# 5120 small memsets on an idle GpSimd, beside a kernel that stores 520 MB

## The chip, the cores and the metric

One core of a Trainium2 chip (trn2) runs the kernel. The metric is device time in microseconds (us), and the figure quoted for a kernel is the median.

## The reference

For each of 4096 rows and each pair i < j of 32 fields of 64 numbers, field i is multiplied by the 64x64 matrix of that pair and then, number by number, by field j.

```python
vi = inputs[:, i_idx, :]            # 496 pairs i < j
vj = inputs[:, j_idx, :]
vdotw = jnp.einsum('bpd,pde->bpe', vi, W)
inter = vdotw * vj
return inter.reshape(B, -1)         # 4096 x 31744, float32: 520 MB
```

## The kernel before

All matrices stay in SBUF. For each of 32 tiles of 128 rows, x is loaded and transposed (ScalarE evicts the transposes), TensorE multiplies into PSUM, VectorE multiplies the PSUM result by x into a ring in SBUF, and SyncE issues four stores from the ring. GpSimd does nothing after the start.

```python
for t in range(NT):
    xt = xbuf[t % 2]
    if t + 1 < NT:
        load_x(t + 1)                     # one DMA on ScalarE's queue
    for s, group in enumerate(STORES):    # four stores a tile
        osb = ring[:, at : at + store_w[s]]
        ...
        for p in group:
            ...                           # transposes of the next x
            for c1 in range(first, width[2 * p] + 1, BANK):
                ...                       # 40 turns in a tile
                pm = take_banks(2)
                for h in range(1 + bool(odd)):
                    nc.tensor.matmul(pm[...], xT[...], w_sb[...], start=True, stop=True)
                nc.vector.tensor_tensor(osb..., pm..., xj, ALU.mult)
        nc.sync.dma_start(out=out[ts(t, P), o0 : o0 + store_w[s]], in_=osb)
```

Of the kernel before, what the change touches and what calls it, by code (L numbers as in the profile page):

```python
# [1 line left out]

# [6 lines left out]

F32 = mybir.dt.float32  # L10
ALU = mybir.AluOpType

P = 128
BANK = 512
BANKS = 8

STORES = [[0, 1], [2, 3], [4, 5, 6], [7, 8, 9, 10, 11, 12, 13, 14, 15]]

LOADS = [[0], [1], [2, 3], [4, 5, 6], [7, 8, 9, 10, 11, 12, 13, 14, 15]]


FIRST_HALF_AT, SECOND_HALF_AT = 9, 3
RING = 28160


@with_exitstack
def pair_bilinear_kernel(
    ctx: ExitStack,
    tc: tile.TileContext,
    x: bass.AP,  # L30
    w: bass.AP,
    out: bass.AP,
    F: int,
    D: int,
):























    nc = tc.nc
    NT = x.shape[0] // P  # L60
    NPR = F // 2

    width = [(F - 1 - i) * D for i in range(F)]
    off = [sum(width[:i]) for i in range(F)]


    woff = [i % 2 * D + sum(width[i % 2 : i : 2]) for i in range(F)]
    store_w = [sum(width[2 * p] + width[2 * p + 1] for p in g) for g in STORES]

    const = ctx.enter_context(tc.tile_pool(name="const", bufs=1))  # L70
    psum = ctx.enter_context(tc.tile_pool(name="ps", bufs=1, space=bass.MemoryType.PSUM))

    ident = const.tile([P, P], F32, tag="ident", name="ident")
    make_identity(nc, ident)

    def runs(tl, a, b, n):

        ap = tl[:, a : a + n]
        return bass.AP(ap.tensor, ap.offset, [list(ap.ap[0]), [b - a, 2], list(ap.ap[1])])

    xbuf = [const.tile([P, F * D], F32, tag=f"x{b}", name=f"x{b}") for b in range(2)]

    def load_x(t):
        nc.scalar.dma_start(out=xbuf[t % 2], in_=x[ts(t, P), :])

    pring = psum.tile([P, BANKS * BANK], F32, tag="pring", name="pring")
    bank = 0

    def take_banks(n):

        nonlocal bank
        if bank + n > BANKS:
            bank = 0
        got = pring[:, bank * BANK : (bank + n) * BANK]
        bank = (bank + n) % BANKS
        return got

    xT = const.tile([P, NPR * P], F32, tag="xT", name="xT")

    def transpose_x(xt, g):  # L100

        n = 2 * BANK // P
        pt = take_banks(2)
        for c in range(n):
            nc.tensor.transpose(pt[:, ts(c, P)], xt[:, ts(n * g + c, P)], ident)  # L105
        nc.scalar.copy(xT[:, ts(g, 2 * BANK)], pt)  # L106

    ring = const.tile([P, RING], F32, tag="ring", name="ring")
    at = 0

    load_x(0)
    w_sb = const.tile([P, sum(width[0::2])], F32, tag="w", name="w")
    done = 0
    for g in LOADS:

        upto = woff[2 * g[-1]] + width[2 * g[-1]]
        nc.sync.dma_start(out=w_sb[:, done:upto], in_=w[:, done:upto])
        done = upto

    transpose_x(xbuf[0], 0)  # L120
# [3 lines that stand above are left out]
            load_x(t + 1)  # L124
        for s, group in enumerate(STORES):
            if at + store_w[s] > RING:
                at = 0
            osb = ring[:, at : at + store_w[s]]
            at += store_w[s]
            o0 = off[2 * group[0]]  # L130
            for p in group:
                if p == SECOND_HALF_AT:
                    transpose_x(xt, 1)
                if p == FIRST_HALF_AT and t + 1 < NT:
                    transpose_x(xbuf[(t + 1) % 2], 0)
                first = (width[2 * p] - 1) % BANK + 1
                for c1 in range(first, width[2 * p] + 1, BANK):
                    n = first if c1 == first else BANK
                    c0 = c1 - n
                    odd = width[2 * p + 1] and c1 > D  # L140
                    pm = take_banks(2)
                    for h in range(1 + bool(odd)):
                        a = woff[2 * p + h] + c0 - h * D
                        nc.tensor.matmul(  # L144
                            pm[:, h * BANK : h * BANK + n],
                            xT[h * D : (h + 1) * D, ts(p, P)],
                            w_sb[h * D : (h + 1) * D, a : a + n],
                            start=True,
                            stop=True,
                        )  # L150
                    xj = xt[:, (2 * p + 1) * D + c0 : (2 * p + 1) * D + c1]
                    o = [off[2 * p + h] - o0 + c0 - h * D for h in range(2)]
                    if odd and (c0 or c1 < width[2 * p]):
                        nc.vector.tensor_tensor(  # L154
                            runs(osb, o[0], o[1], n),
                            runs(pm, 0, BANK, n),
                            bass.AP(xj.tensor, xj.offset, [xj.ap[0], [0, 2], xj.ap[1]]),
                            ALU.mult,
                        )
                    else:  # L160
                        for h in range(1 + bool(odd)):
                            nc.vector.tensor_tensor(  # L162
                                osb[:, o[h] + h * D : o[h] + n],
                                pm[:, h * (BANK + D) : h * BANK + n],
                                xj[:, h * D :],
                                ALU.mult,
                            )
            nc.sync.dma_start(out=out[ts(t, P), o0 : o0 + store_w[s]], in_=osb)


# [26 lines left out]
```

## Time and profile before

| | before |
|---|---|
| time | 1338.01 us (1337.81 to 1338.14) |
| VectorE busy | 1183.0 us, 89% |
| TensorE busy | 1164.7 us, 87% |
| GpSimd busy | 0.7 us |
| DMA engines | over 90% in 39 of 40 slices, 421 GB/s |
| VectorE waits for stores | 101.6 us |

A busy share near 90% on two engines is no bound while both wait. The row to look for is the one without gaps, and that is the transfers. The prediction below shows these lines. One view that it doesn't show is used later, the same kernel in three stretches of 408 us (columns: stretch, length, busy time and count of PE, PEld, DVE, ACT and POOL, then granted clock, DMA share, GB/s):

```profile
100.00:508.00 408.00, 360.62 (x1674) 172.59 (x1676) 367.39 (x429) 20.24 (x20) 0.00 (x0) 0.95 0.99 424
508.00:916.00 408.00, 363.75 (x1674) 175.35 (x1676) 367.64 (x428) 20.24 (x20) 0.00 (x0) 0.95 0.99 424
916.00:1324.00 408.00, 355.62 (x1644) 165.96 (x1640) 365.37 (x426) 19.23 (x19) 0.00 (x0) 0.97 0.99 423
```

### The profile page before, as it was taken

The numbers are of one execution on the slowest core, as the hardware profiler recorded it, in microseconds if no ns is written. First come the engines' busy times: TensorE is split into PE (matmuls) and PEld (weight loads), VectorE is DVE, ScalarE is ACT, GpSimd is POOL, SyncE is SP. The second block draws the span as 40 slices with busy tenths as digits, with TensorE's granted clock in tenths as the row PEclk, the third lists the DMA queues.
The fourth block names the chain that finished last, engine by engine and source line by source line (L and its number), as shares of the span: only waits on it lengthen the run. The fifth ranks groups of instructions, "written<-read, shape, count | busy, mean of one in ns | idle before, by whom it ended". The sixth has DMA issues, their size and how long they took to land.

```text
span 1336.3 us, 13134 instructions
## 1 busy us (share of the span) xinstructions
PE 1164.7 (87%) x5376; PEld 552.9 (41%) x5376; DVE 1183.0 (89%) x1376; ACT 66.1 (5%) x65; POOL 0.7 (0%) x6
## 2 busy tenths in 40 slices
PE   6988888988889888898888898888988888898893
PEld 3444344443444444344434444444444444443341
DVE  5999888989889988999988899888998888998894
ACT  0000000000000000000000000000000000000000
POOL 0000000000000000000000000000000000000000
PEclk9999999999999988998998999889988989999997
DMA  9999999999999999999999999999999999999998
GB/s 395 431 428 436 429 425 427 425 425 425 426 421 401 425 431 415 427 421 425 429 428 419 417 416 435 421 415 425 422 422 426 423 424 412 431 412 439 417 424 353
DMA packets 23820, 562.88 MB, mean 421 GB/s; under 512 B 2640, under 2 KB 2640, under 8 KB 2896
## 3 DMA queue, kind: packets, MB, share of 16 engines
q1 hardware_dynamic: 19152, 528.49, 92.6%
q10 hardware_dynamic: 4608, 33.56, 6.0%
q8 instruction: 42, 0.69, 0.2%
q14 instruction: 18, 0.15, 0.0%
HBM read 41.94 MB, written 520.09 MB: 421 GB/s over the span
## 4 chain that ended last, share of the span: by engine, by line
DMA 45%; DVE 36%; PE 9%; issue 8%; DVEq 0%; ACT 0%
DMA out_dram<-ring 45%; DVE ring L154 30%; PE pring L144 9%; DVE ring L162 5%; DMA x<-in_x_dram 1%; DVEq L154 0%; PE pring L105 0%; ACT xT L106 0%; DVEq L193 0%
## 5 line engine op out<-in xcount | busy, mean ns | idle before, releaser
L144 PE MATMUL pring<-w,xT 64*128 64x512 f32 (+4 forms) x4864 | 1102.6, 568 | 143.3 <-DVE ring L154 131.8
L154 DVE TENSOR_TENSOR ring<-pring,x 128x1024 f32<-128x1024 f32 (+3 forms) x1056 | 1104.6, 1107 | 135.3 <-DMA out_dram<-ring 101.6
L144 PEld LDWEIGHTS pring<-w,xT 64*128 64x128 f32 x4864 | 497.3, 194 | 706.5 <-DVE ring L154 508.4
L106 ACT COPY xT<-pring 128x1024 f32<-128x1024 f32 x64 | 64.8, 1012 | 1225.5 <-PE pring L105 1183.7
L162 DVE TENSOR_TENSOR ring<-pring,x 128x64 f32<-128x64 f32 (+3 forms) x320 | 97.6, 355 | 0.3
L105 PEld LDWEIGHTS pring<-ident,x 128*128 128x128 f32 x512 | 55.6, 142 | 57.1 <-DVE ring L154 48.5
L105 PE MATMUL pring<-ident,x 128*128 128x128 f32 x512 | 70.9, 282 | 8.7 <-DMA x<-in_x_dram 8.7
L106 ACT ACT_TABLE_LOAD x1 | 1.3, 1283 | 1.6 <-PEq L189 1.6
masks.py:199 POOL TENSOR_SCALAR_AFFINE_SELECT ident<-ident 128x128 f32<-128x128 f32 x1 | 0.3, 292 | 0.1
masks.py:197 POOL MEMSET ident<- 128x128 f32 x1 | 0.2, 204 | 0.3 <-POOLq L189 0.3
L189 POOL MEMSET const-bfloat16-1.0<- 128x1 bf16 x1 | 0.1, 101 | 0.0
L189 POOL MEMSET const-uint8-127<- 128x1 uint8 x1 | 0.1, 101 | 0.0
L189 POOL MEMSET const-float32-0.0<- 128x1 f32 x1 | 0.1, 98 | 0.2 <-issue 0.2
L189 POOL MEMSET const-float32-1.0<- 128x1 f32 x1 | 0.1, 98 | 0.0
## 6 DMA issues: line engine op xcount, KB each, us to landing
out_dram<-ring SPq DMA_DIRECT2D x32, 4896.0 KB, 19.5
out_dram<-ring SPq DMA_DIRECT2D x32, 3936.0 KB, 17.7
out_dram<-ring SPq DMA_DIRECT2D x32, 3776.0 KB, 19.6
out_dram<-ring SPq DMA_DIRECT2D x32, 3264.0 KB, 20.1
x<-in_x_dram ACTq DMA_DIRECT2D x32, 1024.0 KB, 18.1
w<-in_w_dram SPq DMA_DIRECT2D x1, 2592.0 KB, 26.1
w<-in_w_dram SPq DMA_DIRECT2D x1, 2016.0 KB, 19.8
w<-in_w_dram SPq DMA_DIRECT2D x1, 1664.0 KB, 15.5
```

The lines of the kernel that those rows point to most:

```text
L105: nc.tensor.transpose(pt[:, ts(c, P)], xt[:, ts(n * g + c, P)], ident)
L106: nc.scalar.copy(xT[:, ts(g, 2 * BANK)], pt)
L144: nc.tensor.matmul(pm[:, h * BANK : h * BANK + n], xT[h * D : (h + 1) * D, ts(p, P)], w_sb[h * D : (h + 1) * D, a : a + n], start=True, st ...
L154: nc.vector.tensor_tensor(runs(osb, o[0], o[1], n), runs(pm, 0, BANK, n), bass.AP(xj.tensor, xj.offset, [xj.ap[0], [0, 2], xj.ap[1]]), ALU ...
L162: nc.vector.tensor_tensor(osb[:, o[h] + h * D : o[h] + n], pm[:, h * (BANK + D) : h * BANK + n], xj[:, h * D :], ALU.mult,)
L189: nc = bacc.Bacc("TRN2", target_bir_lowering=False, num_devices=1)
```

## The change

Its intent is to give the idle engine work that no other engine depends on: four memsets of one spare column in each of the 1280 turns of the inner loop.

```diff
     ring = const.tile([P, RING], F32, tag="ring", name="ring")
+    spare = const.tile([P, 1], F32, tag="spare", name="spare")
...
                     pm = take_banks(2)
+                    for _ in range(4):
+                        nc.gpsimd.memset(spare, 0.0)
```

## The prediction

> **What bounds the kernel now.** I read the page from the top: busy shares, the slices, the chain that ended last, then the waits, and last a table of the four tiles around the middle.

> ```profile
> span 1336.3 us, 13134 instructions
> PE 1164.7 (87%) x5376; PEld 552.9 (41%) x5376; DVE 1183.0 (89%) x1376; ACT 66.1 (5%) x65; POOL 0.7 (0%) x6
> DMA  9999999999999999999999999999999999999998
> ...
> HBM read 41.94 MB, written 520.09 MB: 421 GB/s over the span
> DMA out_dram<-ring 45%; DVE ring L154 30%; PE pring L144 9%; DVE ring L162 5%; DMA x<-in_x_dram 1%; DVEq L154 0%; PE pring L105 0%; ACT xT L106 0%; DVEq L193 0%
> ```

> The DMA row is full in 39 of 40 slices, and no engine is. The chain that ended last spends 45% of the span in the stores of the ring and most of the rest in VectorE's products (L154 and L162): a product may overwrite a piece of the ring only when the store of that piece has landed. Who waits for whom, in the listing of waits:

> ```profile
> DVE ring L154 <- DMA out_dram<-ring: 101.6, 40, 4.1
> DVE ring L154 <- PE pring L144: 22.8, 16, 13.6
> ```

> VectorE waits 101.6 us in all for stores, in 40 waits of at most 4.1 us, and only 22.8 us for TensorE, of which 13.6 are the start. So the stores set the pace and VectorE is close behind. The stretches of 41 us, nearly one tile of 128 rows each, say it by tile (columns: stretch, length, busy time and count for PE, PEld, DVE, ACT and POOL, then clock, DMA share, GB/s):

> ```profile
> 641.00:682.00 41.00, 35.82 (x170) 15.95 (x168) 36.99 (x43) 2.02 (x2) 0.00 (x0) 1.00 1.01 430
> 723.00:764.00 41.00, 36.19 (x166) 18.42 (x166) 36.97 (x43) 2.02 (x2) 0.00 (x0) 0.92 0.99 422
> ```

> VectorE works 36.97 us of a tile's 41 and TensorE about 36. Each has 4 to 5 us of air in a tile, the transfers have none, GpSimd has all of it. The clock granted to TensorE moves between 0.92 and 1.00 without moving the tile. Only three things could therefore cost time: something that takes VectorE more than its air, something that slows the transfers, or GpSimd ending last.

> **What the change really issues.** In the built program, the streams of TensorE, VectorE, ScalarE and SyncE are instruction for instruction what they were, waits included. GpSimd gets 5120 memsets of 128x1 float32. "Without waiting" isn't what was built: 5119 of them wait for GpSimd's own semaphore to reach the count that the memset before them sets, because all write the same column. They wait for no other engine, and nobody waits for them but the barrier at the end. So they form one serial chain that starts at once and runs at its own pace, and the pace decides if it ends before the rest.

> **The pace of the chain.** GpSimd's timeline at the start has both cases:

> ```profile
> 0.24 0.10 POOL L189 MEMSET const-float32-0.0<- 128x1 f32 x1 [0.24 <-issue]
> 0.27 0.10 POOL L189 MEMSET const-float32-1.0<- 128x1 f32 x1
> 0.31 0.10 POOL L189 MEMSET const-bfloat16-1.0<- 128x1 bf16 x1
> 0.34 0.10 POOL L189 MEMSET const-uint8-127<- 128x1 uint8 x1
> 0.73 0.20 POOL masks.py:197 MEMSET ident<- 128x128 f32 x1 [0.29 <-POOLq L189]
> 1.01 0.29 POOL masks.py:199 TENSOR_SCALAR_AFFINE_SELECT ident<-ident 128x128 f32<-128x128 f32 x1
> ```

> Memsets without a wait start 0.03 us apart though each shows 0.10: they overlap, and 5120 of them would be gone in 5120 x 0.033 = 0.17 ms. The select in the last line waits for the memset above it, as each new memset waits for its predecessor: start to start 0.28 us for a memset of 0.20. A one-column memset is 0.10 shorter (0.10 against 0.20), so a step of the new chain should be 0.28 - 0.10 = 0.18 us. 5119 x 0.18 = 921 us, and with 1 us of start GpSimd is done at about 922 us, 414 us before the end. It would end last only with a step over 1335 / 5119 = 0.261 us. This estimate rests on one pair of instructions, the second of another kind and with a register move between; I give a step over 0.26 us some 4%.

> [...]

> [...]

> [...] 10752 instructions (5376 matmuls and 5376 weight loads) x 64 B = 688,128 B, which is the 0.69 MB in 42 packets of the first queue below.

> ```profile
> q8 instruction: 42, 0.69, 0.2%
> q14 instruction: 18, 0.15, 0.0%
> ```

> **The change part by part.** Removed: nothing. Moved: the resident weights by 32 bytes in SBUF, to make room for the column. They are loaded once[...]; 0 us.

> Added, busy time: 5120 x 0.10 = 512 us of GpSimd shown busy (38%), beside everything; 0 us on the path. With start and end of a memset overlapping nothing in the chain, that is what the page should count.

> Added, VectorE: 0 ns for each memset[...]. The air allows some: 101.6 us / 5120 = 19.8 ns for each memset before VectorE takes over as the bound.

> Added, transfers: 5120 x 64 B = 327,680 B of instructions, 0.06% of the 562.88 MB moved. At 421 GB/s this is 0.8 us if it spreads over the 16 DMA engines, and this is time on the path, since the transfers are the bound.

> Sum: 1337.94 + 0.8 = 1338.7 us, rounded to 1339.

> **The rivals.** First, the lock: each memset might hold VectorE off for its 0.10 us. Then VectorE gains 512 us, less the 102 it waits for stores: 410 us more, about 1748. [...] A partial form, say 30 ns each, makes 154 us, less 102: some 52 us, 1390. I give these 1.5% together.

> Second, GpSimd as the bound: a step of 0.30 us makes 5119 x 0.30 = 1536 us, and the kernel some 1540. [...]

> Third, one DMA engine rather than sixteen. The trace has the 16 landing marks of each transfer, one from each DMA engine: the last comes a median of 2.1 us after the fifteenth, while most of the others lie within 0.2 us. So one engine is behind, and a store has landed only when it has. In the trace before, an instruction packet of 8 KiB took 0.309 us in most cases; the new fetches are 40 of them, 12.4 us of one engine's time if they all use the same one. If that is another than the late engine, the time stays where it is; if it is the late one, it is +12 us at worst, 1350, still inside 2%. I take one chance in eight.

> Fourth, the clock: more engines at work could lower TensorE's granted clock. But TensorE at 36 of 41 us has room for over 10%, and the tiles above take the same 41 us at 0.92 and 1.00. 0 us.

> **Range and chances.** The unchanged core of the argument gives 1338 to 1340. Executions of the kernel before scatter by only 0.3 us[...]: low end 1336. The high end, 1346, takes in part of the third rival. Slower by over 2% (above 1364.7) needs the lock or a step over 0.26 us: 1.5 + 4, about 5%. Faster has no mechanism at all: 1%. Within 2%: 94%.

> **What would show it.** Right: POOL with 5126 instructions and near 512 us busy, its digits ending about slice 28 of 40 (922 / 33.4 us each); the product of 1024 columns still at 1217 ns; the waits of VectorE for stores still near 100 us; the instruction queue up by 0.33 MB. Wrong: POOL digits up to the last slice and a chain led by POOL (the step is too short here); L154 above 1217 ns with fewer waits for stores (the lock); 8 to 12 us more with L154 unchanged and more waiting for stores (the late DMA engine).

The 0 ns for VectorE stands as my guess, not shown before the result; the trace before couldn't test it, as GpSimd is idle there while VectorE works. "The lock" is my name for the rival that a memset holds VectorE off. The low end of 1336 is an allowance of mine. The 64 B of an instruction are the trace's: 0.69 MB for 10752 instructions. That a landing mark comes from one DMA engine is my reading: the trace before has 165 transfers and 2640 marks, 16 each.

## The result and the profile after

The changed kernel takes 1354.38 us (1354.19 to 1354.46), 16.4 us more than the 1338.01 of before. The ratio is 1.0122, with a 95% interval of 1.0105 to 1.014. The time lies within 2%, but outside the range of 1336 to 1346 that I had given.

The page of the changed kernel, the lines that answer to those shown of before:

```profile
span 1352.6 us, 18254 instructions
PE 1161.6 (86%) x5376; PEld 553.5 (41%) x5376; DVE 1182.5 (87%) x1376; ACT 66.1 (5%) x65; POOL 503.6 (37%) x5126
POOL 6666666666666666666666640000000000000000
q14 instruction: 58, 0.48, 0.1%
DMA out_dram<-ring 51%; DVE ring L159 29%; DVE ring L167 5%; PE pring L149 5%; POOL spare L146 0%; DVEq L159 0%; PE pring L107 0%; ACT xT L108 0%; DVEq L198 0%; POOL ident masks.py:199 0%; DVEq L167 0%; POOL ident masks.py:197 0%; POOLq L194 0%
```

GpSimd ends in slice 24 of 40, so it doesn't end last, and it is on 0% of the chain. The stores' share of the chain rose from 45% to 51%. L154 of before is L159 here. Its widest form, from the groups with shapes kept apart (row: busy us, mean ns, idle before), and the wait for stores, from the listing of waits (us in total, times, longest):

```profile
L159 DVE TENSOR_TENSOR ring<-pring,x 128x1024 f32<-128x1024 f32 x768 | 901.8, 1214 | 17.3 <-PE pring L149 4.2 <-DMA out_dram<-ring 2.1
DVE ring L159 <- DMA out_dram<-ring: 122.0, 45, 5.0
```

A product takes 1214 ns against 1217 before: VectorE isn't slowed. It waits 122.0 us for stores against 101.6, which is 20.4 us more; this is where the time shows up. The same three stretches as before:

```profile
100.00:508.00 408.00, 351.85 (x1634) 167.82 (x1634) 358.54 (x416) 20.24 (x20) 256.89 (x2615) 0.95 0.98 417
508.00:916.00 408.00, 355.32 (x1638) 171.21 (x1638) 361.41 (x423) 19.23 (x19) 183.82 (x1871) 0.95 0.98 415
916.00:1324.00 408.00, 361.86 (x1682) 171.91 (x1680) 369.43 (x432) 20.24 (x20) 0.00 (x0) 0.96 0.99 422
```

Look at the last column beside the POOL column. While the memsets run, the transfers move 415 to 417 GB/s instead of 424, and when they have ended, 422. The loss is 1.9% of some 800 us, 15 us. So while the memsets run it is the transfers that lose time, and not an engine's work. The granted clock is unchanged (0.954 over the run against 0.956).

GpSimd's timeline at the start gives the pace of the chain:

```profile
0.72 0.20 POOL masks.py:197 MEMSET ident<- 128x128 f32 x1 [0.29 <-POOLq L194]
0.87 0.10 POOL L146 MEMSET spare<- 128x1 f32 x1
1.00 0.29 POOL masks.py:199 TENSOR_SCALAR_AFFINE_SELECT ident<-ident 128x128 f32<-128x128 f32 x1
1.23 4.78 POOL L146 MEMSET spare<- 128x1 f32 x31
```

31 memsets take 4.78 us, 0.154 us each; over all of them the start-to-start spacing is 0.156 us, and the last starts at 799.8 us.

### The profile page after: what moved, and what is told of

Same layout as the page of the kernel before. It is cut to its first block, busy times and chain, and to the rows that moved or that the text cites. A ratio compares the mean times of both kernels' runs of the same rounds, so it can differ in the third digit from the quotient of the medians.

```text
span 1352.6 us, 18254 instructions
## 1 busy us (share of the span) xinstructions
PE 1161.6 (86%) x5376; PEld 553.5 (41%) x5376; DVE 1182.5 (87%) x1376; ACT 66.1 (5%) x65; POOL 503.6 (37%) x5126
## 2 busy tenths in 40 slices
DMA  9999999999999999999999999999999999999998
DMA packets 23860, 563.21 MB, mean 416 GB/s; under 512 B 2640, under 2 KB 2640, under 8 KB 2896
## 3 DMA queue, kind: packets, MB, share of 16 engines
q10 hardware_dynamic: 4608, 33.56, 5.9%
HBM read 41.94 MB, written 520.09 MB: 416 GB/s over the span
## 4 chain that ended last, share of the span: by engine, by line
DMA 51%; DVE 34%; issue 9%; PE 5%; POOL 0%; DVEq 0%; ACT 0%; POOLq 0%
DMA out_dram<-ring 51%; DVE ring L159 29%; DVE ring L167 5%; PE pring L149 5%; POOL spare L146 0%; DVEq L159 0%; PE pring L107 0%; ACT xT L108 0%; DVEq L198 0%; POOL ident masks.py:199 0%; DVEq L167 0%; POOL ident masks.py:197 0%; POOLq L194 0%
## 5 line engine op out<-in xcount | busy, mean ns | idle before, releaser
L159 DVE TENSOR_TENSOR ring<-pring,x 128x1024 f32<-128x1024 f32 (+3 forms) x1056 | 1103.5, 1105 | 150.9 <-DMA out_dram<-ring 122.0
L146 POOL MEMSET spare<- 128x1 f32 x5120 | 503.0, 98 | 295.8
```

Of the source, the lines that this page charges most:

```text
L146: nc.gpsimd.memset(spare, 0.0)
L159: nc.vector.tensor_tensor(runs(osb, o[0], o[1], n), runs(pm, 0, BANK, n), bass.AP(xj.tensor, xj.offset, [xj.ap[0], [0, 2], xj.ap[1]]), ALU ...
```

## The experiments

**The theories.** A: the 327,680 B of GpSimd instructions are fetched by the one DMA engine that is behind the others, and every store waits for it. B: GpSimd's writes to SBUF, or its being busy, disturb VectorE or the transfers. After the first four runs theory A became A2: each instruction that is executed, whatever it does, loads that one DMA engine. All runs gave correct results. Differences are against the median of the kernel before in the same group of runs: 1338.07, 1338.18, 1338.14 and 1338.17 us. Instructions that do nothing were to stand in for the memsets, but plain no-ops were gone from the built program; drains stay (run 13 has 18254 instructions, 5120 more than the 13134 of before), so drains were used.

**1. Instructions that write nothing (e1_pool_drain).**

```diff
-                        nc.gpsimd.memset(spare, 0.0)
+                        nc.gpsimd.drain()
```

> 5120 drains on GpSimd in place of the memsets: as many instructions to fetch, but nothing is written to SBUF and no semaphore is counted up. Theory A (the 327,680 B of GpSimd instructions are fetched by the DMA engine that is late anyway, and every store waits for it): about 1354 us, the same 16 us more (1350 to 1358), with the second instruction queue near 0.48 MB. Theory B (the writes to SBUF or the semaphore updates disturb VectorE or the transfers): 1338 to 1340 us.

Measured: 1350.50 us (1350.09 to 1350.78), 12.4 us more, ratio 1.0092. So most of the loss, 12.4 of 16.4 us, needs no write, no time that the page counts as busy on GpSimd (0.7 us, as before) and no semaphore: 2.43 ns for each drain. Theory B in its pure form falls.

**2. The same writes from a loop (e2_pool_loop).** Four columns, so that a turn needs no waits inside it, and one drain a turn to keep the turns apart. A copy from the identity matrix only sets the order at the start.

```diff
-                    for _ in range(4):
-                        nc.gpsimd.memset(spare, 0.0)
...
     transpose_x(xbuf[0], 0)
+    with tc.tile_critical():
+        with nc.gpsimd.Fori(0, 1280) as _i:
+            for c in range(4):
+                nc.gpsimd.memset(spare[:, c : c + 1], 0.0)
+            nc.gpsimd.drain()
```

> 5120 memsets of one column each, but in a loop of 1280 times four on GpSimd, so the instructions are fetched once. Theory A: 1338 to 1340 us, the second instruction queue back near 0.15 MB. Theory B: 1350 to 1358 us, since as much is written. If a loop turn fetches its instructions anew, the queue shows it and the run says nothing.

Measured: 1357.61 us (1357.51 to 1357.79), 19.5 us more, ratio 1.0147. From its page:

```profile
span 1355.6 us, 22106 instructions
q14 instruction: 18, 0.15, 0.0%
```

The instruction queue is back at 0.15 MB, so nothing was fetched anew, and still this is the dearest of the variants on GpSimd. Theory A falls: it isn't the fetched bytes. But the first line has 22106 instructions, 8972 more than before. A turn of the loop executes seven: four memsets, the drain, an addition and a branch, and 1280 x 7 = 8960. 19.5 us over 8972 is 2.18 ns, close to the 2.43 ns of a drain in the run above. That points to the number of executed instructions, and this became theory A2. The run doesn't separate the kinds: 5120 memsets at the 3.20 ns of the change and 1280 drains at 2.43 make 19.5 us as well, with nothing for the additions and branches. Against that reading, these memsets post no semaphore updates (the kept trace has 5945 in all, against 11059 in the changed kernel), and run 13 suggests that the update is a part of the 3.20.

**3. The same number on another engine (e3_sp_drain).**

```diff
-                        nc.gpsimd.memset(spare, 0.0)
+                        nc.sync.drain()
```

> 5120 drains on SyncE, 160 in each tile between the stores that it issues; GpSimd idle. Theory A in its wide form (all engines' instructions but TensorE's come over the same late DMA engine): about 1354 us. Theory A in its narrow form (each sequencer fetches over a DMA engine of its own, and GpSimd's is the late one): 1338 to 1342 us. Theory B: 1338 to 1342 us too.

Measured: 1373.09 us (1372.86 to 1373.30), 35.0 us more, ratio 1.0261, beyond either theory. This run isn't clean: with the drains in SyncE's stream, the scheduler put TensorE's instructions in another order. From the waits of this run:

```profile
DVE ring L159 <- PE pring L149: 48.6, 46, 13.6
```

VectorE waits 48.6 us for TensorE, against 22.8 before. How the 35 us divide between the drains and the new order stays open.

**4. Half the dose (e4_half).** `range(4)` becomes `range(2)`: 2560 memsets.

> 2560 memsets instead of 5120. Theory A and theory B both say half of the 16.4 us: 1346 us (1344 to 1348). If the loss does not scale (a shift in the phase of stores and products, or the place of the weights in SBUF), it is nearer to 1338 or to 1354.

Measured: 1345.92 us (1345.81 to 1346.14), 7.9 us more, ratio 1.0059. It scales: 3.07 ns for each memset here, 16.37 / 5120 = 3.20 ns in the full change. From a shift of phase or of addresses I would not expect a half.

**5. Few wide memsets (e5_wide).**

```diff
-    spare = const.tile([P, 1], F32, tag="spare", name="spare")
+    spare = const.tile([P, 2048], F32, tag="spare", name="spare")
...
         xt = xbuf[t % 2]
+        for _ in range(13):
+            nc.gpsimd.memset(spare, 0.0)
...
-                    for _ in range(4):
-                        nc.gpsimd.memset(spare, 0.0)
```

> 416 memsets of 2048 columns in place of 5120 of one: GpSimd is busy about as long (416 x 1.8 us = 0.75 ms) and writes 166 times as much into SBUF, with a twelfth of the instructions. Theory A2 (each instruction that is executed costs the transfers about 2.3 ns, by what it sends over the late DMA engine's path, whatever it does): 416 x 3.2 ns = 1.3 us, 1339 to 1341 us. Theory B (GpSimd's writes or its being busy disturb): at least 1350 us.

Measured: 1339.46 us (1339.38 to 1339.55), 1.3 us more, ratio 1.0010. The group of these memsets on the page:

```profile
L127 POOL MEMSET spare<- 128x2048 f32 x416 | 751.2, 1806 | 23.8
```

GpSimd is busy for 751.2 us, longer than in the change itself, and writes 166 times as much, and it costs 1.3 us: 3.08 ns for each of the 416, though the interval of the ratio, 0.9995 to 1.0025, takes in no change at all. This is the cleanest of the runs against theory B.

**6 and 7. Splitting the load of x (e6_x120, e7_x126).** The aim was to take load off some DMA engines. What the traces show of how a transfer is shared out: each of the 165 transfers of the kernel before leaves 16 packets of 4 bytes and 16 landing marks, 2640 of each. The extra loads of runs 9, 14 and 11 below, of 68, 85 and 34 rows, leave 4, 5 and 2 more small packets each: the page's packets under 512 B rise from 2640 to 2764, 2795 and 2702, which is by 31 x 4, 31 x 5 and 31 x 2. I read each of these packets as one DMA engine taking part. Which engines these are, no record names, and for runs 6, 7 and 10 no count is shown here. So the engine numbers in the expectations are labels of mine: 0 to k-1 are the k engines of one extra load, 15 or 14 and 15 those that the split was meant to relieve, 0 to 7 those meant to get a row more. That a smaller set is part of a larger one, and that the split relieves any engine, I assumed; it was not shown.

```diff
-        nc.scalar.dma_start(out=xbuf[t % 2], in_=x[ts(t, P), :])
+        for lo, hi in ((0, P),) if t < 2 else ((0, 120), (120, P)):
+            nc.scalar.dma_start(out=xbuf[t % 2][lo:hi, :], in_=x[t * P + lo : t * P + hi, :])
```

> The kernel before without memsets, but from the third tile on x is loaded as 120 rows and 8 rows. [...] Theory A2 with engine 15 as the late one: faster, 1310 to 1330 us. With one of 8 to 14 as the late one: 1338 us. With one of 0 to 7: 30 x 0.3 = 9 us more, 1347 us. If no engine is late by load: 1338 to 1347 us.

> As the run with 120 rows, with 126 rows[...] Late engine 14 or 15: faster, 1310 to 1330 us. Late engine another: 1345 to 1357 us.

The edit of the second run is the same, with 126 for 120. Measured: 1349.23 us (1349.05 to 1349.77) with 120 rows, 11.1 us more, ratio 1.0083; 1347.53 us (1347.29 to 1347.84) with 126, 9.4 us more, ratio 1.0070. Neither run is faster, so if the split relieved an engine, nothing was gained by it. As an estimate, a packet of 8 KB, one row of x, took 0.309 us (median of the 4096 in the trace before), so one row more in each of 30 tiles on the engine that comes last would cost 30 x 0.309 = 9.3 us, near the losses; that the split puts one there was not shown. In both runs a tile also has one transfer more than before, and what that costs by itself was not measured apart; run 9 below, which has one more too, costs 6.9 us. Which engine is late, these two runs don't tell.

**8. The same number on ScalarE (e8_act_drain).** `nc.scalar.drain()` in place of the memset.

> 5120 drains on ScalarE, most of them in the first ten tiles; GpSimd idle. Theory A2 (any engine's instructions cost alike): 12 to 16 us more, 1350 to 1355 us, or some more if the drains delay the copies of x. If only GpSimd's cost: 1338 to 1340 us.

Measured: 1348.60 us (1348.38 to 1348.86), 10.4 us more, ratio 1.0078, or 2.04 ns for each drain. That is under the 12 to 16 us expected, but of the kind: it isn't a property of GpSimd.

**9, 10 and 14. Finding the late DMA engine (e9_extra4, e10_extra6, e14_extra5).** The kernel before, with one unused load a tile: 68, 102 or 85 rows of 1 KB, meant for four, six or five engines, 17 KB for each. For four and five the count of small packets above bears it out. The 0.65 us for 17 KB are an estimate from 0.309 us for 8 KB.

```diff
-        nc.scalar.dma_start(out=xbuf[t % 2], in_=x[ts(t, P), :])
+        ld = nc.scalar.dma_start(out=xbuf[t % 2], in_=x[ts(t, P), :])
+        if t:
+            with tc.issue_after(ld.ins):
+                nc.scalar.dma_start(out=extra, in_=x[0 : 68, 0:256])    # 102, 85
```

> The kernel before without memsets, plus one small unused load a tile: 68 rows of 1 KB[...], 17 KB to each, about 0.65 us of its time. If one late engine sets the pace and is 2 or 3: 31 x 0.65 = 20 us more, 1358 us. If it is 4 to 7 (engines 0 to 3 have room for it): 1338 to 1341 us.

> The same with 102 rows of 1 KB[...]. Late engine 2 to 5: about 1358 us. Late engine 6 or 7: 1338 to 1341 us. If both this and the run with four engines cost nothing or cost in proportion to their bytes (68 KB and 102 KB of 17.3 MB a tile, 5 and 8 us), no single engine sets the pace and theory A2's late engine is refuted.

> The small unused load[...] (85 rows of 1 KB). Late engine 4: about 1360 us, as with engines 0 to 5. Late engine 5: about 1345 us, as with engines 0 to 3.

Measured: 1344.99 us with the load for four engines (two runs, 1344.30 to 1345.68), 6.9 us more, ratio 1.0052. For six 1359.93 (1359.70 to 1360.17), 21.8 us more, ratio 1.0163. For five 1359.70 (1359.63 to 1359.77), 21.5 us more, ratio 1.0161. ScalarE's DMA queue on the page of the run with four, and below it of the run with five:

```profile
q10 hardware_dynamic: 6840, 35.72, 6.4%
```

```profile
q10 hardware_dynamic: 7398, 36.26, 6.5%
```

The run with four was a miss: neither 1338 to 1341 us nor 1358. Before, this queue has 4608 packets. 31 x (68 + 4) = 2232 and 31 x (85 + 5) = 2790 are just what came on top: rows, and one small packet for each engine. From four to five engines the bytes rise by 0.54 MB, or 0.1% of all, and the time by 14.7 us. From five to six it rises by 0.2 us. If the five are the four and one more, which was not shown, that one (4 in the labels) sets the pace of the whole kernel. As an estimate, the four then have room for 21.5 - 6.9 = 14.6 us over the run, though not for all of what they were given. Two more things weaken this: four engines are a power of two and five and six are not, and no run with eight was made to tell this apart; and run 14 was on another chip than runs 9 and 10, though the kernel before took 1338.14 and 1338.17 us on the two.

**11 and 12. Making other engines late (e11_heavy2, e12_heavy2_memset).** As above with 34 rows of 4 KB, which leave two small packets a load, so over two engines (0 and 1 in the labels), without the memsets and with them.

```diff
+                nc.scalar.dma_start(out=extra, in_=x[0 : 34, 0:1024])
```

> The kernel before without memsets, plus an unused load a tile of 34 rows of 4 KB[...], 68 KB or 2.6 us to each. This makes these two the late ones: slower than 1338 us by 31 x (2.6 us less their room now, which I put at 0.5 to 1.5 us), 1370 to 1400 us. It is the reference for the next run.

> The run before with the 5120 memsets of the change. If what the memsets cost falls on the one engine that was late (theory A2, an engine other than 0 and 1), it is now hidden behind engines 0 and 1: at most 2 us more than the run without memsets. If the memsets slow all transfers or another part, the whole 16 us come on top.

Measured: 1400.39 us (1399.94 to 1400.85) without memsets, 62.3 us above the kernel before, ratio 1.0465, and 1400.73 us (1399.35 to 1401.22) with all 5120 of them, ratio 1.0466. The first is at the upper edge of what was expected. The memsets cost 0.3 us here, less than the scatter. The first two stretches without memsets, then with:

```profile
100.00:508.00 408.00, 342.75 (x1572) 164.42 (x1572) 347.16 (x403) 19.24 (x19) 0.00 (x0) 0.94 0.96 407
508.00:916.00 408.00, 350.12 (x1616) 170.76 (x1616) 354.39 (x415) 19.23 (x19) 0.00 (x0) 0.95 0.95 405
```

```profile
100.00:508.00 408.00, 343.74 (x1572) 168.34 (x1574) 347.38 (x402) 19.23 (x19) 257.87 (x2604) 0.93 0.96 407
508.00:916.00 408.00, 350.15 (x1614) 172.15 (x1612) 353.84 (x414) 19.23 (x19) 186.71 (x1885) 0.95 0.95 405
```

The POOL column is full in the second pair, and the rates are equal. If the memsets slowed all transfers, the loss would be here too. It hides behind the two engines that the extra load makes late, so it doesn't fall on these two. A loss in VectorE would hide as well, since VectorE waits 151.3 us for stores in run 11; against that one speaks the product of 1024 columns, 1217 ns in both runs.

**What the landing marks say.** Each of the 165 transfers of the kernel before leaves 16 landing marks in the kept trace, in the changed kernel too (2640 in each), and in order of time they can be read by stretch. In run 11 the last two come 0.07 us apart (median), and the third from last 5.8 us before the last: two late engines, as many as the extra load leaves small packets. From 60 us on until the extra instructions end, the last mark trails the one before it by 3.3 us in the changed kernel (the kernel before, same stretch: 2.0), 4.2 in run 1 (1.3), 3.8 in run 2 (2.0) and 3.2 in run 8 (1.8). After they have ended it is 2.8 (2.3), 2.0 (2.3), 2.5 (2.3) and 1.2 (2.3). So while the instructions run, one engine drops behind the fifteen others: the load doesn't spread. The marks don't name the engine. In run 13 below it is two marks that drop back: the fifteenth is 1.6 us before the last (1.8), the fourteenth 4.2 (2.6).

**13. The semaphore update (e13_drain_update).** The drains of run 1, each with an update that nobody waits for.

```diff
-                        nc.gpsimd.drain()
+                        nc.gpsimd.drain().then_inc(count, 1)
```

> 5120 drains on GpSimd as before, but each counts a semaphore up that nobody waits for. If every semaphore update costs the late DMA engine something of its own (0.8 ns, from the difference between the memsets and the drains): 5120 x (2.43 + 0.77) ns = 16.4 us more than before, 1354 us (1352.5 to 1356). If the difference came from the memsets' writes or their slower pace: 1350.5 us as without updates (1349.5 to 1351.5).

Measured: 1354.03 us (1353.86 to 1354.24), 15.9 us more, ratio 1.0119. That is 3.10 ns for each drain against 2.43 without an update, so an update would cost about 0.7 ns, and of the memset's 3.20 ns only 0.1 ns is left for its write and all else. But the update also slows the drains, from 61 to 96 ns from start to start, and the pace is not separated from it: ScalarE's drains, 33 ns apart, cost 2.04 ns, and the memsets, 156 ns apart, 3.20. Only run 2 breaks that order, with 77 ns from one instruction to the next and 2.18 ns.

**What stays open.** What an executed instruction sends to the late DMA engine, and why this engine. The recording itself is a candidate: the traces hold an entry for each instruction and one for each semaphore update (18254 and 11059 in the changed kernel, 13134 and 5940 before), and a cost for each entry would fit one for each instruction and a smaller one for each update. But no run here was made without recording, so this is a guess of mine, not shown, and an unrecorded execution may lose less or nothing. No version that beats the kernel before was found. By theory A2 it would be one with fewer executed instructions; an attempt at fewer for TensorE did not compile.

## Why the prediction was wrong, by its own steps

- **What bounds the kernel.** Right as far as it went: the stores. It stopped at sixteen DMA engines taken together. The landing marks show that one of them comes last (2.1 us after the fifteenth in the median before), and the step of 14.7 us from run 9 to run 14 fits one that sets the pace while others have room.
- **The chain of 5120 memsets.** Right in kind. The step measured 0.156 us against 0.18, so GpSimd was done at 800 us rather than 922. Its busy time was 503.6 us against 512.
- **VectorE, 0 ns for each memset.** Right: 1214 ns against 1217 for the widest product. Run 5 measures it with 751.2 us of memsets beside the products: the widest stays at 1217 ns.
- **The clock.** Right: the mean granted clock is 0.954 against 0.956. But that the tiles "take the same 41 us" at 0.92 and 1.00 reads a length that was set by hand; what shows it is that both stretches hold 43 products.
- **The transfers, the step that failed.** The prediction put in "0.8 us if it spreads over the 16 DMA engines", counting fetched bytes, and 16.4 us came. The bytes came as worked out (0.48 against 0.15 MB), but the load neither spreads nor consists of them. It falls on one engine (the landing marks: the last trails by 3.3 us while the memsets run, 2.0 before; by run 12 not on the two of the extra load), it remains when nothing is fetched (run 2), and it measures 5120 x 2.43 = 12.4 us for executed instructions, plus 5120 x 0.77 = 3.9 us that come with the semaphore updates, or with the slower pace that they bring. The 0.77 ns is the rest that makes 16.4; run 13 measured 0.67 ns of its own.
- **The third rival.** It had the place, one late DMA engine, and gave it one chance in eight. Its cause was wrong, and so was its limit: 40 packets of 0.309 us can't cost more than 12.4 us, and 16.4 came. That run 1's drains cost 12.4 us as well is a coincidence, as run 2 shows. The sign that the prediction named for it came, the product unchanged and more waiting for stores, with 16.4 us in place of 8 to 12. The reading it rested on, that the last landing mark trails by a median of 2.1 us, was a true hint. Over the whole run this lag is no measure (2.9 us in the changed kernel, 1.7 us in run 8, which lost 10.4 us); taken only while the instructions run, it grows in both.
